# A gated cross-attention and feed-forward network on one core: the opening of stage 0 rearranged, and every product of stage 6 put into a fixed order

## The chip, the cores and the metric

The kernel runs on one core of one Trainium2 chip. The metric is device microseconds for one execution. The core's engines are called here as the profile calls them: PE is TensorE (matrix products and transposes), PEld its weight loads, DVE VectorE, ACT ScalarE, POOL GpSimd, SP SyncE, which here only issues DMAs. Each engine runs its own instructions in order; semaphores tie them together. PSUM, where products land, has eight banks of 128 x 512 float32.

## What is computed

The input x is 4 batches of 512 rows of 512 numbers, with a context of 4 x 512 rows of 256. Four pairs of blocks, eight stages (0 to 7), are added to x one after the other, each gated by tanh of a number:

```
x = x + tanh(g_xattn[0]) * L0_xattn(layernorm(x), ctx)     # stage 0
x = x + tanh(g_ffn[0])   * L0_ffn(layernorm(x))            # stage 1
...
x = x + tanh(g_xattn[3]) * L3_xattn(layernorm(x), ctx, pos) # stage 6
x = x + tanh(g_ffn[3])   * L3_ffn(layernorm(x))            # stage 7
```

Stage 0 is an attention with 16 heads of 32. Queries come from x, keys and values from the first 496 rows of the context, and queries and keys are normalized head by head. The last 16 rows of the context have weights of their own and a softmax of their own (the short context), and both results are added:

```
q = _ln((x @ Wq + bq).reshape(b, s1, H, HD), qn_w, qn_b)
k = _ln(kv[..., :HD], kn_w, kn_b)
ctx = _attn(q, k, v)
ctx_dca = _attn(q, k_dca, v_dca)        # 16 rows
return (ctx + ctx_dca) @ Wo + bo
```

Stage 6 is an attention with 32 heads of 16 over 512 context rows, with rotary positions on queries and keys, and an output product.

## The kernel before

Everything is float32 but for small helpers; the rows of x stay in SBUF for the whole run, as 16 tiles of 128 x 512. The stages follow each other; `tile_blocks_kernel` (L1873) opens a set of buffer pools for each.

**Who decides the order.** The code emits instructions in one order. A scheduler then places each engine's instructions when the kernel is built, by priority (what is emitted earlier, or under `high_priority`, comes first) and by its own idea of when inputs are ready. `tie` (L244) is the kernel's own means against that: a tied product may not be placed ahead of the tied product emitted before it. `together` (L253) emits a group of products, tied, to run side by side in different row or column groups of PE's array; the first of them may be made to wait for other instructions (`after`), so that the group starts as a whole. A `chain` (L235) is a sum of products into one bank; it is tied only if told so.

**Stage 0** (`s0`, L272). First the loads: SP issues, in the order of the code, the gates' numbers, the context of batch 0, the weights for keys and values (`wkv`), their bias, `wq`, `bq`, the short context's weights `wd` and bias, `wo`, `bo`, small rows, and six vectors of 32 numbers (`nw32`). The 16 tiles of x are issued by ACT (L70). `centre` (L319) subtracts from each head's weights their mean, on DVE, so that the normalization needs no mean. A product of `nw32` (L306) spreads the normalization's weights over the partitions.

`pieces(b)` (L351) lists the preparation of a batch: `kv` (four steps: keys and values of 128 rows), `xT` (layernorm and transposes of x), `turned` (transposes of normalized keys or queries), `query` (two steps), and `short` and `shortT` (logits, softmax and transposes of the short context). `second` (L490), called by batch 0's `short`, makes the short context's keys (`kbd`) and values (`vbd`). For batch 0 all pieces stand before the attention; for later batches they are dealt out over the slots of the batch before.

`maxima` (L555) is a generator. Each step gives a pair of products whose row maximum DVE takes (`after`); a head group of four heads and 512 queries takes eight steps. LEAD = 12 steps run ahead, as pairs (L681). Then each of the 32 slots of a batch (L685) joins two logit products (`pl`), the next pair of maxima (`ps`), a correction by the maxima, an exponential on ACT, and, one slot later, products with the values (`av`) or the sums (`sm`). The pool `sc` has two buffers of two banks, `pl` one of two banks, `av` and `sm` one bank each.

**Stage 6** (`s6`, L1534) is built in the same way, with 64 slots for each batch: two `pl`, two `ps`, and half of a step of `av` (`weigh`, L1687). After the last `av` of a head group ACT copies it out, and `norm` (L1710) transposes and scales it; after the last group `project` and `projected` make the output rows. `turn` (L1630) transposes the maxima into spare rows of the queries. `results`, `xT`, `query`, `queryT` are the next batch's preparation; `results` adds stage 5's outcome to x, which is 32 long additions on DVE in all. Banks come from two rings, four of `sc` and three of `pl`; `dealt` (L1553) remembers the reader of a bank for the groups, while `bank` (L1563) deals without remembering it. Only the groups of `together` are tied; transposes and chains are free.

Of the kernel before, what the change touches and what calls it, by code (L numbers as in the profile page):

```python
# [48 lines left out]
class Net:  # L49


    def __init__(self, ctx, tc, a):
# [10 lines left out]
        nc.sync.dma_start(self.gx, a["g_xattn"].partition_broadcast(P))  # L63
        nc.sync.dma_start(self.gf, a["g_ffn"].partition_broadcast(P))

        self.x = []
        for b in range(NB):
            for t in range(b * TB, (b + 1) * TB):
                xt = self.const.tile([P, D], F32, name=f"x_{t}")
                nc.scalar.dma_start(xt, a["x"][t * P : (t + 1) * P, :])  # L70
                self.x.append(xt)
# [39 lines left out]
        nc.scalar.activation(self.gx, self.gx, AF.Tanh)  # L111
        nc.scalar.activation(self.gf, self.gf, AF.Tanh)
# [45 lines left out]
    def evict(self, i, out, in_):  # L158

        if i % 2:  # L160
            self.nc.scalar.copy(out, in_)  # L161
        else:
            self.nc.vector.tensor_copy(out, in_)
# [60 lines left out]
    def transposed(self, name, src, dst, i=0, tied=False, room=None):  # L224

        pt = (room or self.mm)(f"ptr_{name}")
        for c in range(4):
            ins = self.nc.tensor.transpose(  # L228
                pt[:, c * P : (c + 1) * P], src[:, c * P : (c + 1) * P], self.ident
            ).ins  # L230
            if tied:
                self.tie(ins)
        self.evict(i, dst, pt.rearrange("p (c n) -> p c n", c=4))
# [38 lines left out]
    def s0(self):  # L272
# [8 lines left out]
        nc.sync.dma_start(wkv, a["s0_wkv"].rearrange("(c p) n -> p c n", p=P))  # L281
        bk = self.bcast("s0_bk", a["s0_bkv"][0:512])
        nc.sync.dma_start(wq, a["s0_wq"].rearrange("(c p) n -> p c n", p=P))
        bq = self.bcast("s0_bq", a["s0_bq"])
        nc.sync.dma_start(wd, a["s0_wd"].rearrange("(c p) n -> p c n", p=P))
        bd = self.t("s0_bd")
        nc.sync.dma_start(bd, a["s0_bd"][0:512].partition_broadcast(P))
        nc.sync.dma_start(wo, a["s0_wo"].rearrange("(c p) n -> p c n", p=P))
        bo = self.bcast("s0_bo", a["s0_bo"])
        fixed = lambda name, shape, dtype=F32: self.gp.tile(shape, dtype, tag=name, name=name)  # L290
# [4 lines left out]
        nc.vector.tensor_tensor(bvs[:, 0, :], bvs[:, 0, :], bvs[:, 1, :], op=ALU.add)  # L295
        bv = bvs[:, 0, :]

        nw32 = fixed("s0_nw32", [HD, 6])
        for i, k in enumerate(("qn_w", "qn_b", "kn_w", "kn_b", "kn_dca_w", "kn_dca_b")):
            nc.sync.dma_start(nw32[:, i : i + 1], a[k].rearrange("(p o) -> p o", o=1))  # L300
# [4 lines left out]
        pn = self.sc("s0_pn")[:, 0, 0:6]  # L305
        nc.tensor.matmul(  # L306
            pn, lhsT=rep.rearrange("p r m -> p (r m)"), rhs=nw32, start=True, stop=True
        )
        nw = fixed("s0_nw", [P, 6])
        nc.vector.tensor_copy(nw, pn)  # L310
        nc.vector.tensor_scalar(nw[:, 0:2], nw[:, 0:2], HD**-0.5, None, op0=ALU.mult)
# [20 lines left out]
        centre("wq", wq.rearrange("p c (h d) -> p c h d", d=HD))  # L332
        centre("bq", heads(bq))
# [17 lines left out]
        def pieces(b):  # L351
# [15 lines left out]
            def kv(k):  # L367
# [3 lines left out]
                for i in range(2):  # L371
                    self.chain(
                        pkv[:, i, :],
                        [
                            (cx[:, c, k * P : (k + 1) * P], wkv[:, c, i * 512 : (i + 1) * 512])
                            for c in range(CC)
                        ],
                    )
# [4 lines left out]
                if k == TB - 1:  # L383
                    normed(f"s0k_{b}", heads(room["k"]), room["vk"])
# [36 lines left out]
            def query(y):  # L421
# [21 lines left out]
                if y == 1:  # L443
                    normed(f"s0q_{b}", heads(room["q"]), room["vq"])

            def short():

                if b == 0:
                    second()
# [22 lines left out]
            def shortT():  # L472
# [7 lines left out]

            return (
                [lambda k=k: kv(k) for k in range(TB)]
                + [lambda y=y: xT(y) for y in range(2)]
                + [lambda y=y: turned("k", y, kT, 2) for y in range(2)]
                + [lambda y=y: query(y) for y in range(2)]
                + [lambda y=y: turned("q", y, qT, 0) for y in range(2)]
                + [short, shortT]
            )

        def second():  # L490


            n = NB * ND
            cd = fixed("s0_cd", [P, CC, NB, ND])
            for c in range(CC):
                nc.sync.dma_start(
                    cd[:, c],
                    a["ctxT"][c * P : (c + 1) * P, :].rearrange("p (b n) -> p b n", b=NB)[:, :, M:S],
                )
            centre("wd", wd[:, :, 0:512].rearrange("p c (h d) -> p c h d", d=HD))  # L500
            centre("bd", heads(bd))
            pk = self.sc("s0_pkd")[0:n, 0, :]
# [3 lines left out]
            kd = self.t("s0_kd")[0:n]  # L506
            va = self.s("s0_vd", H)[0:n]
            nc.vector.tensor_tensor(kd, pk, bd[0:n], op=ALU.add)
            squares("s0d", kd, va, n)
            normed("s0d", heads(kd), va, n)  # L510
            pt = self.sc("s0_ptd")[:, 0, 0 : 4 * n].rearrange("p (g b k) -> p b g k", g=4, b=NB)
            for g in range(4):
# [3 lines left out]
                    self.ident[0:n, 0:n],  # L516
# [23 lines left out]
            vbd = fixed("s0_vbd", [P, NB, D])  # L540
            for b in range(NB):
                pv = self.sc(f"s0_pvd_{b}")[:, 0, :]
                self.chain(
                    pv,
                    [
                        (cr[:, c, b].rearrange("p r k -> p (r k)"), wd[:, c, 512:1024])
                        for c in range(CC)
                    ],
                )
                nc.vector.tensor_tensor(vbd[:, b, :], pv, mask, op=ALU.mult)  # L550
            made["kbd"], made["vbd"] = kbd, vbd

        maxT = {}

        def maxima():  # L555

            freed = []
# [19 lines left out]
            for b in range(NB):  # L577
                kT, qT = made[b][0:2]
                for g in range(4):
                    nmx = self.s(f"s0_nmx_{b}_{g}", 16, "s0_nmx")  # L580
                    for t in range(TB):
                        for y in range(2):
# [3 lines left out]
                            ps = self.sc(f"ps_s0_{b}_{g}_{t}_{y}")  # L586
# [88 lines left out]
        for b in range(NB):  # L675
            stats[b] = self.lnstats(f"s0_{b}", self.x[b * TB : (b + 1) * TB], b)
            if b == 0:
                for piece in pieces(0):
                    piece()
        beside = maxima()  # L680
        for _ in range(LEAD):  # L681
            parts, freed, after = next(beside)
            self.together(parts, freed)
            after()
        for b in range(NB):  # L685
            kT, qT = made[b][0:2]
            todo = pieces(b + 1) if b + 1 < NB else []
# [730 lines left out]
    def rope(self, name, ps, t, out):  # L1418

        nc = self.nc  # L1420
# [3 lines left out]
        for i in range(2):  # L1424
# [3 lines left out]
            nc.vector.tensor_tensor(dst, x[:, 0, :, :], (cos, sin)[i], op=ALU.mult)  # L1428
            nc.vector.tensor_tensor(dst, dst, tmp, op=(ALU.subtract, ALU.add)[i])

# [12 lines left out]
    def headsT(self, name, r, y, pt):  # L1443

        v = r.rearrange("p (g h) k -> p g (h k)", g=8)
        for i in range(4):
            self.nc.tensor.transpose(pt[:, i * P : (i + 1) * P], v[:, 4 * y + i, :], self.ident)
# [86 lines left out]
    def s6(self):  # L1534
# [18 lines left out]
        def dealt(name, tag="sc"):  # L1553
            at = len(readers[tag])
            readers[tag].append(None)
            old = readers[tag][at - banks[tag]] if at >= banks[tag] else None
            t = self.ps3.tile([P, S], F32, tag=tag, name=f"s6_{name}", bufs=banks[tag])
            return t, (tag, at), [old] if old is not None else []

        def read(where, ins):  # L1560
            readers[where[0]][where[1]] = ins
# [434 lines left out]
```

## Time and profile before

| | us |
|---|---|
| median of 3 runs | 3382.92 (3382.7 to 3385.21) |
| the profiled execution | 3387.32 |
| its span | 3385.4 |
| first product of PE | starts at 32.27 |
| first product of keys (`s_pkv`) | 32.75 |
| first query product (`s_pq`) | 57.81 |
| first maxima (`ps_s`) | 111.39 |
| first logits (`pl_s`), stage 0 | 132.68 |
| batches 0, 1, 2, 3 of stage 0 begin | 132.68, 274.76, 434.55, 592.35 |
| stage 6 | about 2254 to 3003 |

The profile is of one execution, 4.4 us longer than the median of the runs. Times in a timeline are microseconds from the start of the span, then the duration; in square brackets stands the idle time of the engine before the instruction, and what ended it. A line with "x4" is four instructions merged. One float32 product appears as two records. In the table of windows each engine has its busy time and the number of its instructions, then come the granted clock of PE (1.00 is full), the share of the DMA engines' time, and GB/s. `s_` in front of a name is the stage's prefix with its number left out, so stage 0 and stage 6 both have an `s_po`.

### The profile page before, as it was taken

The numbers are of one execution on the slowest core, as the hardware profiler recorded it, in microseconds if no ns is written. First come the engines' busy times: TensorE is split into PE (matmuls) and PEld (weight loads), VectorE is DVE, ScalarE is ACT, GpSimd is POOL, SyncE is SP. The second block draws the span as 40 slices with busy tenths as digits, with TensorE's granted clock in tenths as the row PEclk, the third lists the DMA queues.
The fourth block names the chain that finished last, engine by engine and source line by source line (L and its number), as shares of the span: only waits on it lengthen the run. The fifth ranks groups of instructions, "written<-read, shape, count | busy, mean of one in ns | idle before, by whom it ended". The sixth has DMA issues, their size and how long they took to land.

```text
span 3385.4 us, 41976 instructions
## 1 busy us (share of the span) xinstructions
PE 2917.4 (86%) x15644; PEld 1452.6 (43%) x15648; DVE 1972.4 (58%) x3132; ACT 1196.0 (35%) x1927; POOL 626.0 (18%) x509
## 2 busy tenths in 40 slices
PE   4889898967998889998845699978999999989994
PEld 2333333223444444443423588853333333254673
DVE  5555555548898988886678311138656566634103
ACT  2243333355554454433322111113545444520231
POOL 0000000005564655660000122210000000000351
PEclk9799999988998999999967699987999999999997
DMA  3000000047676886861222599971000000022698
GB/s 126 7 1 7 1 1 9 1 157 223 197 230 183 235 231 194 235 207 61 79 72 73 183 320 324 323 272 47 14 27 13 27 1 1 1 75 78 247 385 315
DMA packets 266346, 438.69 MB, mean 130 GB/s; under 512 B 32368, under 2 KB 114544, under 8 KB 264608
## 3 DMA queue, kind: packets, MB, share of 16 engines
q1 hardware_dynamic: 247776, 382.52, 35.9%
q0 software_dynamic: 13760, 45.10, 3.7%
q10 hardware_dynamic: 4608, 8.39, 0.7%
q8 instruction: 125, 2.05, 0.3%
q14 instruction: 77, 0.63, 0.1%
HBM read 370.79 MB, written 65.13 MB: 129 GB/s over the span
## 4 chain that ended last, share of the span: by engine, by line
PE 37%; DVE 7%; issue 4%; ACT 2%; POOL 2%; DMA 2%; SPq 0%; POOLq 0%; ACTq 0%; DVEq 0%
PE s_po L238 8%; PE s_pl L262 8%; PE pg_s L238 6%; PE s_av L262 2%; PE s_pq L238 2%; PE s_ps L262 2%; ACT pr_s L1786 2%; PE s_ph L238 2%; POOL s_ys L1321 1%; DMA s_y<-s_ys 1%; DVE x L729 1%; DVE s_top L1670 1%; POOL s_xb L1294 1%; PE s_pr L238 1%; PE s_pkv L238 1%
## 5 line engine op out<-in xcount | busy, mean ns | idle before, releaser
L1012 POOL TENSOR_TENSOR s_h<-s_h,s_C 128x512 f32<-128x512 f32 x256 | 445.4, 1740 | 298.8 <-DVE s_h L1011 260.3
L1670 DVE TENSOR_REDUCE s_top<-s_ps 128x1 f32<-128x512 f32 x512 | 328.8, 685 | 164.1 <-PE s_ps L262 163.8
L1786 ACT ACTIVATE pr_s<-s_pl 128x512 f32<-128x512 f32 x512 | 277.9, 595 | 327.3 <-PE s_ps L262 293.7
L1011 DVE TENSOR_TENSOR_SCAN s_h<-s_da,s_db 128x512 f32<-128x512 f32 x256 | 311.9, 1218 | 60.1 <-PE s_y L262 34.3
L262 PE MATMUL s_pl<-s_qT,s_kT 32*128 32x512 f32 x1024 | 295.7, 653 | 29.8 <-DVE s_top L1670 11.7
L262 PE MATMUL s_ps<-s_kT,s_qT 32*128 32x512 f32 x1024 | 301.4, 674 | 4.5 <-DVE s_top L1670 4.5
L1010 ACT ACTIVATE s_da<-s_rdl,s_A 128x512 f32<-128x512 f32 x256 | 184.3, 722 | 330.3 <-DVE s_h L1011 327.0
L238 PE MATMUL s_ph<-xT_s,s_wu 128*128 128x256 f32 x1024 | 249.6, 399 | 0.7 <-ACT xT_s L161 0.7
L771 PE MATMUL s_acc<-s_wd,s_hT 128*128 128x512 f32 x512 | 239.9, 612 | 6.8 <-ACT s_hT L802 6.8
L262 PE MATMUL s_av<-pr_s,s_v 128*32 128x256 f32 (+2 forms) x2560 | 238.7, 445 | 0.2
L238 PEld LDWEIGHTS s_ph<-xT_s,s_wu 128*128 128x128 f32 x1024 | 199.3, 199 | 78.1 <-issue 47.7
L238 PEld LDWEIGHTS pg_s<-s_xbT,s_w 128*128 128x128 f32 (+1 forms) x1872 | 214.2, 184 | 19.8 <-issue 17.8
L599 DVE TENSOR_REDUCE s_nmx<-ps_s 128x2 f32<-128x992 f32 x128 | 151.4, 1184 | 116.6 <-PE ps_s L262 116.6
L238 PE MATMUL pg_s<-s_xbT,s_w 128*128 128x128 f32 (+1 forms) x1872 | 215.8, 276 | 1.4 <-ACT s_xbT L161 1.4
L1009 DVE TENSOR_TENSOR s_db<-s_B,s_rdu 128x512 f32<-128x512 f32 x256 | 205.6, 803 | 12.5 <-DMA s_B<-s_bc 4.9
L714 ACT ACTIVATE pr_s<-pl_s 128x1024 f32<-128x1024 f32 (+1 forms) x128 | 130.9, 1023 | 192.1 <-PE pl_s L262 161.7
L262 PE MATMUL s_y<-s_h,ident 64*64 64x512 f32 x1024 | 147.6, 640 | 50.6 <-issue 35.2
L1400 DVE TENSOR_TENSOR g_s<-g_s,pg_s 128x256 f32<-128x256 f32 x78 | 27.5, 352 | 263.8 <-ACT g_s L1399 263.8
L262 PE MATMUL pl_s<-s_qT,s_kT 32*128 32x512 f32 (+1 forms) x512 | 151.1, 668 | 26.1 <-ACT pr_s L714 23.0
L262 PE MATMUL ps_s<-s_kT,s_qT 32*128 32x496 f32 x512 | 156.2, 713 | 4.5 <-DVE s_nmx L599 4.1
L771 PEld LDWEIGHTS s_acc<-s_wd,s_hT 128*128 128x128 f32 x512 | 93.5, 192 | 151.8 <-issue 115.8
L1294 POOL DMA_INDIRECT s_xb<-s_xs,s_from x86 | 83.2, 967 | 378.4 <-PE ptr_s_xb L228 232.4
(376 smaller groups left out, 4264.5 us busy)
## 6 DMA issues: line engine op xcount, KB each, us to landing
s_B<-s_bc SPq DMA_DIRECT2D x256, 256.0 KB
s_C<-s_bc SPq DMA_DIRECT2D x256, 256.0 KB
s_w<-in_s_wg SPq DMA_DIRECT2D x39, 704.0 KB
s_w<-in_s_wu SPq DMA_DIRECT2D x39, 704.0 KB
s_w_rt<-in_s_ru SPq DMA_DIRECT2D x47, 512.0 KB
s_w_rt<-in_s_rd SPq DMA_DIRECT2D x47, 512.0 KB
s_w<-in_s_wd SPq DMA_DIRECT2D x39, 512.0 KB
s_y<-s_ys SPq DMA_DIRECT2D x32, 512.0 KB
```

Source lines behind the costliest of these rows:

```text
L238: ins = self.nc.tensor.matmul(out, lhsT=l, rhs=r, start=(i == 0), stop=(i == len(pairs) - 1)).ins
L262: ins = self.nc.tensor.matmul(out, lhsT=l, rhs=r, **flags).ins
L599: i = nc.vector.tensor_reduce(nmx[:, at : at + 2], ps[:, :, 0:M], axis=AX.X, op=ALU.max, negate=True,)
L714: nc.scalar.activation(prs[i][0:n], pl[0:n], AF.Exp)
L771: ins = nc.tensor.matmul(accs[i][t], lhsT=hT[:, j, t * P : (t + 1) * P], rhs=wd[f // 4][:, f % 4, :], start=(f == 0), stop=(f == FC - 1),).ins
L1009: nc.vector.tensor_tensor(db, br, du, op=ALU.mult)
L1010: nc.scalar.activation(da, dl, AF.Exp, scale=am[:, e, n : n + 1])
L1011: nc.vector.tensor_tensor_scan(h, da, db, 0.0, op0=ALU.mult, op1=ALU.add)
L1012: nc.gpsimd.tensor_tensor(h, h, cr, op=ALU.mult)
L1294: self.nc.gpsimd.indirect_dma_start(out=t, out_offset=None, in_=self.sorted[name][1], in_offset=bass.IndirectOffsetOnAxis(ap=fr[:, j : j + ...
L1670: ins = nc.vector.tensor_reduce(dst[:, i], ps[i][0], axis=AX.X, op=ALU.max, negate=True).ins
L1786: ins = nc.scalar.activation(prs[i][:, j, :], pl[j][0], AF.Exp).ins
```

## The change

In stage 0:

- x is loaded by SP instead of ACT, batch by batch, among the weights: the order is now the context, K's half of `wkv`, its bias, V's half, x of batch 0, `wq`, `bq`, the six vectors, `wd`, the short context's columns, x of batch 1, `wo`, small rows, the gates, x of batches 2 and 3. The gates' tanh goes to `gates`, after that.
- The centring of `wq` and the product of `nw32` become pieces after the four `kv` steps, and batch 0's `kv` chains and that product are tied.
- The normalization of keys and queries is done in halves (`half`), each as soon as two of the four steps are there.
- `second` keeps only the short context's keys before the maxima. Their transposes (`keys`), the four value chains (`values`), and batch 0's `short` and `shortT` become pieces of batch 0's loop.
- The lead of 12 maxima runs as six groups of four heads, two of them in `pl`'s buffer, with one wait for the group.

In stage 6:

- All transposes, query chains (but for batch 0's) and output chains are tied.
- Every deal of a bank remembers its readers, and a group waits for the readers of all banks that it and its neighbours had before (`before`), not for each product's own.
- Three empty pieces follow `results`; `turn`'s addition gets high priority on DVE.

The core of the diff:

```diff
+    def load(self, b):
+        for t in range(b * TB, (b + 1) * TB):
+            self.nc.sync.dma_start(self.x[t], self.a["x"][t * P : (t + 1) * P, :])
+
+    def gates(self):
+        for t, k in ((self.gx, "g_xattn"), (self.gf, "g_ffn")):
+            self.nc.sync.dma_start(t, self.a[k].partition_broadcast(P))
+            self.nc.scalar.activation(t, t, AF.Tanh)
...
-        nc.sync.dma_start(wkv, a["s0_wkv"].rearrange("(c p) n -> p c n", p=P))
-        bk = self.bcast("s0_bk", a["s0_bkv"][0:512])
+        for i in range(2):
+            half = slice(512 * i, 512 * (i + 1))
+            nc.sync.dma_start(
+                wkv[:, :, half], a["s0_wkv"][:, half].rearrange("(c p) n -> p c n", p=P)
+            )
+            if i == 0:
+                bk = self.bcast("s0_bk", a["s0_bkv"][0:512])
+        self.load(0)
         nc.sync.dma_start(wq, a["s0_wq"].rearrange("(c p) n -> p c n", p=P))
         bq = self.bcast("s0_bq", a["s0_bq"])
...
+        self.gates()
+        for b in range(2, NB):
+            self.load(b)
...
-                if k == TB - 1:
-                    normed(f"s0k_{b}", heads(room["k"]), room["vk"])
+                if k % 2:
+                    half("k", k // 2)
...
             return (
                 [lambda k=k: kv(k) for k in range(TB)]
+                + ([weights, lambda: statistics(0), first] if b == 0 else [])
+                + [lambda: turned("k", 0, kT, 2)]
                 + [lambda y=y: xT(y) for y in range(2)]
-                + [lambda y=y: turned("k", y, kT, 2) for y in range(2)]
+                + [lambda: turned("k", 1, kT, 2)]
                 + [lambda y=y: query(y) for y in range(2)]
-                + [lambda y=y: turned("q", y, qT, 0) for y in range(2)]
-                + [short, shortT]
-            )
+                + ([second] if b == 0 else [])
+                + [lambda y=y: turned("q", y, qT, 0) for y in range(2)],
+                [short, shortT],
+            )
...
+        todo, rest = pieces(0)
+        for piece in todo:
+            piece()
+        for b in range(1, NB):
+            statistics(b)
+        alone = [True]
         beside = maxima()
-        for _ in range(LEAD):
-            parts, freed, after = next(beside)
-            self.together(parts, freed)
-            after()
+        for _ in range(LEAD // 2):
+
+            two = [next(beside) for _ in range(2)][::-1]
+            self.together([p for parts, _, _ in two for p in parts], lead[-2:-1])
+            for _, _, after in two:
+                after()
+        alone[0] = False
+        rest = [keys, lambda: values(0)] + rest + [lambda b=b: values(b) for b in range(1, NB)]
...
         def dealt(name, tag="sc"):
-            at = len(readers[tag])
-            readers[tag].append(None)
-            old = readers[tag][at - banks[tag]] if at >= banks[tag] else None
+
             t = self.ps3.tile([P, S], F32, tag=tag, name=f"s6_{name}", bufs=banks[tag])
-            return t, (tag, at), [old] if old is not None else []
...
+            readers[tag].append([])
+            return t, readers[tag][-1].append
+
+        def before(tag):
+
+
+            old = readers[tag][-2 - banks[tag] - 2 : -banks[tag]]
+            return [r[-1] for r in old if r]
...
-            out = [results, lambda: xT(0), lambda: xT(1)]
+            out = [results] + 3 * [lambda: None] + [lambda: xT(0), lambda: xT(1)]
...
-            po = bank(f"pt_{b}_{g}")
+            po, read = dealt(f"pt_{b}_{g}")
             for t in range(TB):
                 ts = slice(t * P, (t + 1) * P)
-                nc.tensor.transpose(po[:, ts], oT[:, ts], self.ident)
+                self.flip(po[:, ts], oT[:, ts], True)
...
-                        self.together(parts + more, freed + pl[0][2] + pl[1][2])
+                        self.together(parts + more, freed + before("pl"))
```

`flip` is a transpose that is tied when told so.

## The prediction

> **What bounds the kernel now.** I read the page's first two parts, then the table of windows over the two stages that the diff touches, then the timelines of their seams.
>
> ```profile
> PE 2917.4 (86%) x15644; PEld 1452.6 (43%) x15648; DVE 1972.4 (58%) x3132; ACT 1196.0 (35%) x1927; POOL 626.0 (18%) x509
> ```
> ```profile
> core 0: us, PE busy (x) PEld busy (x) DVE busy (x) ACT busy (x) POOL busy (x), PEclk, DMA share, GB/s
> 0.00:32.20 32.20, 0.00 (x0) 0.00 (x0) 20.70 (x42) 3.46 (x6) 4.33 (x44) 1.00 0.87 310
> 57.80:111.40 53.60, 36.51 (x114) 19.78 (x114) 21.19 (x27) 10.11 (x15) 1.97 (x3) 0.78 0.00 0
> 111.40:132.70 21.30, 18.93 (x57) 6.21 (x56) 14.18 (x18) 1.01 (x1) 0.00 (x0) 0.50 0.00 1
> 2340.00:3003.00 663.00, 634.92 (x4628) 222.22 (x4624) 392.77 (x681) 312.99 (x580) 0.56 (x3) 0.99 0.03 11
> ```
> TensorE is the bound on the whole, but for the first 32.2 us it does nothing; from 57.8 to 111.4 it is busy for 36.5 of 53.6 us; in stage 6 it is busy throughout, so there only a better packing can gain. The timelines show what each stretch waits for:
>
> ```profile
> 14.81 1.20 DVE L325 TENSOR_REDUCE ce_wk<-s_wkv 128x32 f32<-128x1024 f32 x1
> ...
> 30.37 0.31 SPq L300 DMA_DIRECT2D s_nw<-in_kn_dca_b  x1
> 32.27 0.56 PE L306 MATMUL s_pn<-s_nw,s_rep 32*128 32x6 f32 x2 [32.27 <-DMA s_nw<-in_kn_dca_b]
> ```
> The first product is a tiny one. It waits for six tiny loads queued last behind megabytes, and all keys and values wait behind it.
>
> ```profile
> 2395.64 0.70 PE L262 MATMUL s_pl<-s_qT,s_kT 32*128 32x512 f32 x2
> 2395.65 0.70 PE L262 MATMUL s_ps<-s_kT,s_qT 32*128 32x512 f32 x2
> ...
> 2396.71 0.64 PE L262 MATMUL s_av<-pr_s,s_v 128*32 128x256 f32 x8
> 2397.72 1.13 PE L262 MATMUL s_pl<-s_qT,s_kT 32*128 32x512 f32 x4 [0.37 <-DVE s_top L1670]
> 2398.78 0.33 PE L1716 MATMUL s_pt<-ident,s_oT 128*128 128x128 f32 x1
> 2399.04 1.13 PE L262 MATMUL s_ps<-s_kT,s_qT 32*128 32x512 f32 x4
> 2400.09 0.55 PE L1716 MATMUL s_pt<-ident,s_oT 128*128 128x128 f32 x3
> ```
> In stage 6 a whole slot starts two pl and two ps products together (four row groups, 1.05 us). In a broken one an untied transpose (pt, from norm) sits in the middle: pl alone 1.06, ps alone 1.06. Counting the PE timeline from one start of s_av to the next: 142 plain slots of 1.83 us on average; 27 broken with pt of 3.90, against 2.29 for the three with pt that stayed whole; three with po and broken of 6.69 against 5.27 whole; three with ptx of 8.6 to 11.1.
>
> **Stage 0, until the maxima.** The loads up to K's half of wkv are 1.05 MB. The first x tile (0.26 MB) let DVE start at 4.84; at the 0.39 MB/us of the early DMA slices the rest comes 2.0 later: 6.9. Centring takes 1.20+0.16+1.20, so keys and values begin at 9.5 instead of 32.75. They last 16.0 as before: 25.5. All loads are now issued by SP: ten issues up to wq at about 0.4 are 4 us, hidden under 4 MB of data (0.393 MB/us came on SP's queue alone at 27 to 29 us, so one queue is no slower than two; ACT loses the 16 issues that held it until 20.5). The six tiny loads move ahead of wd and land near 15, before the product that needs them stands in line at 25; cd's two (32 KB, 0.65 to issue each) move ahead of x 1. Without that cover each would hold TensorE as before.
>
> The second limit is DVE, which had 32 idle microseconds for work that now falls beside the keys. After 9.5 it owes, from the rows of before: centring bk 1.5, four key steps of 1.38 (5.5), two half norms of about 1.45 (half of 0.55+2.29; 2.9), wq and bq 6.3, statistics 3.5, xl 2.0, one eviction 1.2; in all 22.9. So the query chain starts near 33, not 57.8. It lasts 14.0: 47. Its second half's norm (add, squares, reduce, root, reciprocal: 4.2 in the row of before, then 1.15 rather than 2.29) ends at 52.3, but the first two groups of maxima need only the first half: 52. ACT and DVE run in order, and gates (two Tanh, with their table loads of 1.28) and the statistics of x 1 to 3 now hang on the last loads, which land at 27 to 31. Stuck ahead of evictions they cost between 0 and 10 here; I take 3, since DVE is the limit until 33 anyway. Maxima begin at 55 instead of 111.4: **-56.5**.
>
> **The lead.** Twelve pairs took 21.3 us (1.66 per pair). Six groups of four wait for the reduce of pl's only buffer, 1.19, then run. The Trainium skill speaks here ("TensorE: Matmul & The Clock Gate", Part 1): after one busy window of about 3.4 us the clock is full. The row 111.4 to 132.7 says otherwise: granted 0.50 through 21 us with PE busy 89% of the time. By the rule a group takes 1.05+0.25+1.19, six take 15, and 6 us are gained; by the row 2.1+0.25+1.19, six take 21, nothing. I take the row: **0**.
>
> **What moves into the first loop.** Keys, four value chains, short and its transposes no longer stand before the maxima; they are seven more pieces among the 20 slots of batch 0. Batches 1 and 2 already show short and shortT beside the loop: the slot with ld takes 5.99 instead of 2.5, the next one 1.0 more, the slot with ptw 10.47, because TensorE waits 3.2 for the softmax chain and the pairs fall apart. That is 12 us, as much as the serial form cost (99.05 to 111.4). Values: 1.72 for each chain plus some 0.3, 8; keys 2. Their DVE work (four multiplies of 0.69, kbd 2.21, two copies of 0.75) fits DVE's 61 idle microseconds in this loop, and the mask (0.52+1.51) stays on an idle POOL. Bounds: 12 if only PE's own time counts (0.7+6.9+3.5+1), 30 if each of seven pieces breaks a slot by another 1.1. I take 22: **+22**.
>
> **Halved norms.** Each batch after the first has four roots instead of two between exponentials, each with two table loads (1.28) and 0.35 on ACT, 2.9. In before such an episode left PE idle for 1.2 where a piece covered it and 3.9 where none did. The six added ones stand before kv (3.7 of PE) and query (7): 0 to 17; I take 3. The shorter multiply takes off some of the three waits of 1.6 before ptk: -2. **+1**.
>
> Stage 0: -33.5. What was hidden there stays hidden: x 1 to 3 are first read after 55.
>
> **Stage 6.** All products in order of emission: norm's four transposes now follow directly on the last weigh, and must wait for ACT's copy of av.
>
> ```profile
> 2374.07 1.09 ACT L1786 ACTIVATE pr_s<-s_pl 128x512 f32<-128x512 f32 x2 [0.72 <-PE s_ps L262]
> 2374.14 0.64 PE L262 MATMUL s_av<-pr_s,s_v 128*32 128x256 f32 x8
> 2375.05 0.59 ACT L1707 COPY s_oT<-s_av 128x512 f32<-128x512 f32 x1
> ```
> The copy stands behind two exponentials and ends 1.5 after av starts, where the next group would start at 0.7. Behind the waiting transposes stands everything on PE. So the slot becomes 1.83+0.46+0.85 = 3.15, not 2.29: the tie gives back half of what it gains. 27x0.75 = -20; five norms without a ps partner lose 0.85: +4; three po slots -4; three ptx slots -13 (the pauses after results give xl time). The other group waits replace waits of the same products; distances shrink where a transposed query deals two tiles (0.1 to 0.2 on twelve), and results' stretch at 2300 to 2340 stays DVE's (18 to 19 busy in 20). Reserve +4. **-29**, bounds -10 and -60.
>
> **Sum**: -33.5-29 = -62.5 on the profiled execution's 3387.3 (span 3385.4 and 1.9 around it): 3324.8. The median of the runs, 3382.9, lies 4.4 lower, so I forecast 3320.
>
> **Rivals.**
> - *Everything is hidden.* norm's copy gets ahead of the exponentials, so slots fall to 2.29 (-27.5 more); the moved pieces cost bare PE time (-10); the lead runs at full clock (-6): 3277. For it: the three whole pt slots. Against: ACT's queue order in the row above.
> - *The new opening waits for its last loads*: Tanh or statistics stand ahead of evictions (+7), the roots cost the uncovered price (+14), stage 6 keeps half (+14): 3355 to 3360. For it: the 3.9 us waits.
> - *Slower*: in-order products make PE wait for its newest input. 126 tied pieces (norm, turn 32 each, xT 6, query and queryT 12 each, project and projected 16 each) need more than 0.5 us of new wait each, beyond norm's, to eat 62.5; at 0.6 it is 3320+76 = 3396. For it: norm itself waits 0.85. Against: the others come a slot (1.8) or more after their source.
> - *No change*: the first product starts early but the query chain stays where it is, and stage 6 trades one wait for another: 3380.
>
> **Chances.** Forecast's case 0.56 (3300 to 3342), all hidden 0.20, late loads 0.18, slower 0.04, no change 0.02. The range 3283 to 3352 leaves out about half of each side case. What this kernel's measurement can tell from no change is about 0.2% (7 us): faster 0.94, same 0.02, slower 0.04.
>
> **What would show it.** First pkv near 9.5, first pq near 33, first ps near 55, first pl near 76; ACT without a long wait for gates. A first pq beyond 40 makes the step on DVE wrong. Batch 0's loop near 164 instead of 142. In stage 6 no pt between pl and ps, pt's slots near 3.1: 2.3 would make the stall wrong, 3.9 the gain.

## The result, and the profile after

The changed kernel takes 3343.07 us (median of 4 runs, 3335.79 to 3345.06) beside 3383.98 for the kernel before: a ratio of 0.9875 [0.9858, 0.9892], 41 us less. The forecast was 3320, its range 3283 to 3352; 3343 is inside the range, just above the 3300 to 3342 that the forecast gave to its own case. The profiled execution took 3345.06 with a span of 3343.2, 42.3 less than the profiled execution before.

In the table of windows of the changed kernel, the first row is the same stretch as before; the others are the lead of maxima, and stage 6 from its first maxima to its last logits.

```profile
core 0: us, PE busy (x) PEld busy (x) DVE busy (x) ACT busy (x) POOL busy (x), PEclk, DMA share, GB/s
0.00:32.20 32.20, 18.85 (x48) 8.71 (x49) 23.18 (x46) 8.01 (x14) 4.33 (x44) 0.98 0.88 288
54.54:76.62 22.08, 14.18 (x61) 5.29 (x61) 16.34 (x23) 3.75 (x6) 0.00 (x0) 0.66 0.00 0
2269.60:2934.70 665.10, 599.01 (x4720) 207.96 (x4724) 432.74 (x783) 320.42 (x592) 0.00 (x0) 0.98 0.05 15
```

The same stretch of stage 6 in the kernel before:

```profile
2291.40:2978.90 687.50, 649.52 (x4721) 224.69 (x4722) 432.59 (x789) 320.90 (x594) 0.00 (x0) 0.97 0.05 15
```

PE works for 18.85 of the first 32.2 us, where it did nothing before. In stage 6 it is now busy for 599 of 665 us, where it was busy for 650 of 687.5. So the products are packed better (51 us less busy time, a few of them the clock's, see below the table), and more than half of what that saved has become waiting (66 us idle instead of 38). The opening's timeline:

```profile
7.32 1.22 DVE L342 TENSOR_REDUCE ce_wk<-s_wkv 128x32 f32<-128x1024 f32 x1 [7.32 <-DMA s_wkv<-in_s_wkv]
...
10.53 8.78 PE L238 MATMUL s_pkv<-s_wkv,ctx_s 128*128 128x512 f32 x16 [10.53 <-DVE s_wkv L344]
...
26.81 0.38 PE L238 MATMUL s_pn<-s_nw,s_rep 32*128 32x6 f32 x2
...
36.62 13.90 PE L238 MATMUL s_pq<-s_wq,s_xT 128*128 128x512 f32 x32
```

The first keys start at 10.53, the tiny product (`s_pn`) stands behind them without a wait, and the query follows at 36.62. A slot of stage 6 with norm's transposes, from one start of s_av to the next:

```profile
2318.80 0.64 PE L262 MATMUL s_av<-pr_s,s_v 128*32 128x256 f32 x8
2318.89 1.08 ACT L1846 ACTIVATE pr_s<-s_pl 128x512 f32<-128x512 f32 x2 [0.72 <-PE s_ps L262]
...
2319.86 0.59 ACT L1765 COPY s_oT<-s_av 128x512 f32<-128x512 f32 x1
...
2320.51 0.66 PE L1495 MATMUL s_pt<-ident,s_oT 128*128 128x128 f32 x4 [1.06 <-ACT s_oT L1765]
```

In all 30 slots with pt and ps the four products of the group now start together, but s_pt waits 1.06 for a copy that stands behind two exponentials on ACT. The list of PE's waits in stage 6 (what waited, for what; us in total, times, longest) gives it as the largest by far:

```profile
PE s_pt L1495 <- ACT s_oT L1765: 29.7, 28, 1.1
PE s_ps L262 <- DVE s_top L1728: 5.8, 4, 1.9
PE s_pl L262 <- ACT pr_s L1846: 5.7, 28, 0.6
PE s_pl L262 <- DVE s_top L1728: 4.0, 4, 1.3
```

The largest line of the same list for the kernel before:

```profile
PE s_pl L262 <- DVE s_top L1670: 11.7, 28, 0.8
```

Nearly all of it stood in the broken slots (one stands in the prediction's timeline, at 2397.72). All lines together are 26.1 us before and 55.7 after.

By stretches of the two profiled executions (us):

| stretch | before | after | difference | forecast |
|---|---|---|---|---|
| up to the first maxima | 111.4 | 54.5 | -56.9 | -56.5 |
| the lead | 21.3 | 22.1 | +0.8 | 0 |
| loop of batch 0 | 142.1 | 164.7 | +22.6 | +22 |
| loops of batches 1 to 3, to stage 1's first product | 446.4 | 449.8 | +3.4 | +1 |
| stage 0 in all | 721.2 | 691.1 | -30.1 | -33.5 |
| stage 6, first maxima to last logits | 687.6 | 665.1 | -22.5 | -29 |
| everything else | 1976.6 | 1987.0 | +10.4 | 0 |

The last line is at least in part scatter. Of the 10.4, stage 1's long stretch has 6.3 (755.4, then 761.7). The kernel with the same stages 0 and 1 but the old stage 6 (first experiment) has 754.1 there, and the twelve kernels below, none of which touches that stretch, lie between 754.0 and 760.7. So single executions differ by some 8 us there, and the two of the table happen to have the shortest and the longest "everything else" of all fourteen profiled executions (1976.6 and 1987.0). The other kernels with the changed stage 0 have 1978.2 to 1986.8, so a few us may be the change's; that was not isolated.

The line of stage 6 needs care as well. Three kernels have stage 6 as it was: the kernel before, and two of the experiments. It takes 687.6, 686.1 and 680.5 us in them. Five kernels have the changed stage 6 as it is, and there it takes 665.1 to 667.5. The granted clock of PE tells the first three apart. The first row below is a stretch in the middle of stage 6 in the kernel before, the second is the same stage in the kernel with 680.5 (the six vectors first), from 2330 to its last logits:

```profile
2678.70:2685.50 6.80, 6.80 (x29) 3.22 (x29) 2.12 (x4) 1.66 (x3) 0.00 (x0) 0.50 0.00 0
2330.00:2966.30 636.30, 611.90 (x4573) 212.83 (x4576) 390.31 (x681) 310.68 (x577) 0.00 (x0) 1.00 0.04 11
```

The kernel before has three such stretches at half clock there, 13.6 us together, and a slot with ptx that falls in part into one takes 11.13, where the same slot takes 9.47 in the other kernel. The changed kernel has none (1.00 from 2312 to its last logits). At half clock products take about twice as long (a group of four 2.04 instead of 1.11, last section), so half of the 13.6 is lost: about the 7 us between 687.6 and 680.5. So of the 22.5 us some 7 are a matter of how the clock fell in one execution, and the change is worth about 15 in stage 6. Below, each edit is read in its own stretch beside the medians.

### The profile page after: what moved, and what is told of

Same layout as the page of the kernel before. It is cut to its first block, busy times and chain, and to the rows that moved or that the text cites. A ratio compares the mean times of both kernels' runs of the same rounds, so it can differ in the third digit from the quotient of the medians.

```text
span 3343.2 us, 42023 instructions
## 1 busy us (share of the span) xinstructions
PE 2877.5 (86%) x15644; PEld 1440.6 (43%) x15648; DVE 1972.4 (59%) x3148; ACT 1215.7 (36%) x1948; POOL 629.3 (19%) x509
## 3 DMA queue, kind: packets, MB, share of 16 engines
q8 instruction: 124, 2.03, 0.3%
## 4 chain that ended last, share of the span: by engine, by line
PE 37%; DVE 7%; ACT 4%; issue 3%; POOL 2%; DMA 2%; POOLq 0%; DVEq 0%; ACTq 0%
PE s_po L238 8%; PE s_pl L262 8%; PE pg_s L238 6%; ACT pr_s L1846 3%; PE s_ph L238 2%; PE s_pq L238 2%; PE s_av L262 1%; DVE x L772 1%; DMA s_y<-s_ys 1%; PE s_pr L238 1%; PE s_pkv L238 1%; PE pt_s L217 1%; POOL s_ys L1364 1%; PE s_pb L238 1%; DVE st_s L174 1%
## 5 line engine op out<-in xcount | busy, mean ns | idle before, releaser
L262 PE MATMUL s_ps<-s_kT,s_qT 32*128 32x512 f32 x1024 | 291.4, 661 | 7.8 <-DVE s_top L1728 5.8
L1052 DVE TENSOR_TENSOR s_db<-s_B,s_rdu 128x512 f32<-128x512 f32 x256 | 202.7, 792 | 13.6 <-DMA s_B<-s_bc 5.9
L262 PE MATMUL pl_s<-s_qT,s_kT 32*128 32x512 f32 (+1 forms) x512 | 154.2, 680 | 26.1 <-ACT pr_s L757 23.0
```

The costliest lines, as they stand in the source:

```text
L262: ins = self.nc.tensor.matmul(out, lhsT=l, rhs=r, **flags).ins
L1052: nc.vector.tensor_tensor(db, br, du, op=ALU.mult)
```

## Experiments

My theory was the prediction's: the two halves of the change are separate, stage 0 is bounded by the path through DVE until the maxima, and in stage 6 the tie of norm's transposes takes back about as much as it gives, because they wait for ACT. The rivals: the moved pieces or the added roots are what costs, and the common wait of a group is what keeps the groups whole. In each entry the ratio is to the kernel before, run on the same chip; the changed kernel's is 0.9875.

**Each half alone.** One kernel has the changed stage 0 and stage 6 as before, the other the reverse.

> Stage 0 of the changed kernel, stage 6 of the kernel before. If the two parts add up, this run is 30 us faster than the kernel before (stage 0 ends at 691 in its trace instead of 721) and its stage 6 takes the 688 us of before between its first maxima and its last logits. The stretch from stage 1's first up-product to its last accumulation grew from 755 to 762 us in the changed kernel's trace, and the router-to-blocks tail by 2. If stage 0's change causes that (other buffers, other times), it stands at 762 here too and the run is only 23 us faster; if it is scatter between executions, it lies anywhere between 754 and 763.

> Stage 6 of the changed kernel, stage 0 of the kernel before. If the parts add up: 21 us faster than the kernel before, all of it between the first maxima and the last logits of stage 6 (665 us instead of 688), and stage 0 ends at 721 as before. If stage 6 gained only because it began at another moment of the clock's throttling, it stays near 680. Stage 1's stretch: 755 if stage 0's change caused the 762, anywhere if it is scatter.

Stage 0 alone: 3357.29 (3347.53 to 3359.65), 0.9914 [0.9899, 0.9929]. Stage 6 alone: 3371.02 (3366.25 to 3381.94), 0.996 [0.9946, 0.9975]. Beside the 3384.5 of the kernel before in these runs they gain 27.2 and 13.5, together 40.7 of the 41: within the scatter the halves do not touch each other. By the stretches they would gain more: 31.4 in stage 0 (689.8) and 20.2 in stage 6 (667.4, beside 687.6). Beside the 680.5 of a stage 6 without the half clock it is 13.1, and that agrees with the median. So stage 6 did not gain only by the moment at which the clock fell, but a third of what the two traces show is that.

**Norm one slot later.**

```diff
                 nc.scalar.copy(oT, avs[g])
+                behind(lambda: None, more=True)
                 behind(norm, b, g, oT, more=True)
```

> The changed kernel, but norm's four transposes are emitted one slot after the copy of av instead of in the same slot. My theory: in the changed kernel the tie makes all of TensorE wait for that copy, 1.07 us in each of 30 slots; a slot later the copy is long done, the slots with pt fall from 3.34 to about 2.29, and the kernel is 30 us faster than the changed one (near 3312). The rival: the 1.07 is the price of the group's wait for DVE's readers, not of the copy. Then the slots with pt stay at 3.3 or the wait moves to the slot after, and the time stays at 3343.

3308.05 (3304.03 to 3313.81), 0.9769 [0.9753, 0.9785]: 36 us less than the changed kernel by the ratios, as expected. Its timeline around the same transposes:

```profile
2319.10 0.59 ACT L1765 COPY s_oT<-s_av 128x512 f32<-128x512 f32 x1
...
2319.85 0.64 PE L262 MATMUL s_av<-pr_s,s_v 128*32 128x256 f32 x8
...
2320.42 0.66 PE L1495 MATMUL s_pt<-ident,s_oT 128*128 128x128 f32 x4
```

The copy is done before the next s_av starts, and s_pt follows without a bracket: no wait. The 30 whole slots with pt last 2.26 on average instead of 3.34, and stage 6 takes 636.8 instead of 665.1. That is 28.3 less, and the wait that it removed was 29.7. (The rest of the 36 lies outside stage 6, mostly in stage 1's stretch: 754.0 beside 761.7.) The waits for exponentials, 5.7 us in 28 places, are gone too (0.7, once): most of them had stood in the slot behind a stall. So the tie cost what it did by the position of the tied instruction.

**Ties without the common wait.** `before` gives no readers, so each product waits only for the reader of its own bank; the ties stay.

```diff
-            return [r[-1] for r in old if r]
+            return []
```

> The changed kernel, but no group of stage 6 waits as a whole: each product waits only for its own bank, and the ties stay. If the ties do the work and the wait only stands in for waits of the same products, it stays within 5 us of the changed kernel (3338 to 3348). If the common wait is what keeps the four products side by side, pl starts ahead of ps in many slots, each of them costs up to 1.05 us more, and with a quarter of some 200 slots that is 50 us slower (3390).

3325.47 (3322.49 to 3326.95), 0.9822 [0.9807, 0.9838]. Neither expectation holds: it is faster, by 18 us. PE's waits in stage 6 of this kernel:

```profile
PE s_pt L1495 <- ACT s_oT L1765: 25.2, 28, 1.1
PE s_ptq L1495 <- DVE s_q_r L1473: 2.1, 1, 2.1
PE s_ps L262 <- DVE s_top L1728: 1.5, 5, 0.5
```

The waits of s_pl for the exponentials and for DVE are gone, and s_ps waits 1.5 in all instead of 5.8. There is a price: in most slots the first product of pl now starts alone, and the other three follow.

```profile
2385.45 0.86 PE L262 MATMUL s_pl<-s_qT,s_kT 32*128 32x512 f32 x2
2385.62 0.70 PE L262 MATMUL s_ps<-s_kT,s_qT 32*128 32x512 f32 x2
```

Of 140 plain slots, 37 start their four products together and take 1.66 on average; 76 start them some 0.17 apart and take 1.83; 27 start them more than 0.2 apart and take 2.17. The changed kernel has 140 together, at 1.88. The stretch of stage 6 goes from 665.1 to 654.7, so 10 us are the common wait's, about half of it in the slots with pt (3.19 instead of 3.34). The rest of the 18 lies where the edit does not reach, mostly in stage 1's stretch (754.0 beside 761.7). I had read the common wait as a mere replacement of each product's own. In the kernel before, too, a group waited as a whole, for those readers of its own banks that `dealt` remembered; so this run shows what a common wait costs, not what the change added to it.

**Own banks only.** Two kernels tell apart the two readings of that: that a group waits for the slowest of its own banks, or that it waits for two banks more (those dealt just before its own). One has the smaller wait, the other has it together with the later norm.

```diff
-            old = readers[tag][-2 - banks[tag] - 2 : -banks[tag]]
+            old = readers[tag][-2 - banks[tag] : -banks[tag]]
```

> The changed kernel with a group waiting only for the last readers of its own banks, not for those of the two banks dealt before them as well. If the common wait costs because every product waits for the slowest of the group's own banks, nothing changes: 3340 to 3347, stage 6 at 665. If it costs because of the two extra readers, it goes to where the kernel without a common wait is: 3325, stage 6 at 655. My theory is the first, because the two extra readers are the older ones.

> Norm one slot later and the common wait only for the group's own banks. With the theory of the run of own banks alone (extra readers cost nothing) it is the same as norm later: 3304 to 3312. With the other it lies at 3290, as norm later without any common wait.

3350.28 (3338.13 to 3352.11), 0.9891 [0.9875, 0.9908], stage 6 at 667.1; and with norm later 3313.26 (3309.55 to 3316.13), 0.9776 [0.976, 0.9793], stage 6 at 635.8. Neither differs from its partner with the larger wait (0.9875 and 0.9769). The medians lie a little above what I wrote, but so does the kernel before in these runs (3387.2). The extra readers cost nothing that can be seen, which leaves the group's own slowest bank.

**Both edits of stage 6.** Norm later, and no common wait.

> The changed kernel with both edits of stage 6 that gained by themselves: norm one slot later and no common wait of a group. Norm later took 35 us off (3308), no common wait 18 (3325). If the two costs are different ones (the transposes' wait for ACT's copy, and a pair held back for the other pair's banks) they add: 3290, stage 6 at 626. If the common wait only cost what it added in the slots that norm's wait had upset, little is left of it: 3303 to 3310.

3301.58 (3296.67 to 3302.86), 0.9742 [0.9726, 0.9758], the best of all. By the ratios it lies 0.0027, or 9 us, below norm later alone, with stage 6 at 629.5 beside 636.8. So 7 to 9 of the common wait's 10 us remain when the slots with pt no longer stall, and perhaps all: this trace has two stretches of 3.4 us at a granted clock of 0.50 in the middle of stage 6, and that of norm later alone has none. Neither expectation was met: the costs are mostly different ones, but the 18 that I added were too many, since some 8 of them were never stage 6's.

**Without the pauses after results.**

```diff
-            out = [results] + 3 * [lambda: None] + [lambda: xT(0), lambda: xT(1)]
+            out = [results] + [lambda: xT(0), lambda: xT(1)]
```

> The changed kernel without the three empty pieces after results. My forecast booked -13 for three ptx slots that wait for xl (8.6 to 11.1 us each before), with the pauses as the reason. Then without them the tied transposes of x wait for xl with everything behind them: three times 3 to 6 us, 3352 to 3361. If it is the tie or the order that gained them, and not the pauses, it stays at 3340 to 3347.

3358.25 (3347.98 to 3361.51), 0.9903 [0.9884, 0.9922]: 9.5 us more by the ratios, 15 more in the stretch of stage 6 (680.2) of the profiled execution, which is the slowest of the four. The six slots with ptx take 46.5 us together, and four of them again carry an output product as well. In the changed kernel the six take 17.3, and the four output products add 13.6 to slots of their own, 30.9 in all. In two of the six, ptx waits 1.40 and 0.73 for xl. Against these 15.6 stand 8 us gained in other slots; and some 7 are lost at the end of the stage, where plain groups take 2.08 instead of 1.13:

```profile
2933.70:2951.50 17.80, 17.80 (x71) 4.41 (x69) 0.68 (x2) 5.43 (x10) 0.00 (x0) 0.50 0.00 1
```

No pause stands near there, so the medians' 9.5 is the better figure for the pauses. They do pay for that part of the stage, by less than the 15.

**Whole norms in stage 0.** K's norm is made after the fourth step and the query's after its second half, so there are two roots for each batch again.

```diff
-                if k % 2:
-                    half("k", k // 2)
+                if k == TB - 1:
+                    normed(f"s0k_{b}", heads(room["k"]), room["vk"])
...
-                half("q", y)
+                if y == 1:
+                    normed(f"s0q_{b}", heads(room["q"]), room["vq"])
```

> The changed kernel with the norms of keys and query undivided again (two roots for each batch instead of four, the multiplies whole). My forecast priced the halving at +1: three for the six added roots, less two for shorter waits ahead of the transposed keys. So undoing it changes nothing that can be told: ratio to the changed kernel within 0.3%, 3334 to 3351 beside 3343, the sqrt table loads of stage 0 back from 25 to 13. The rival of the forecast (the added roots cost their uncovered price) expects 10 to 17 us less: 3326 to 3333. In the opening the second half's norm then stands ahead of the first maxima: first ps 1 to 3 us later than 54.5.

3359.74 (3355.63 to 3362.52), 0.9923 [0.99, 0.9945]. The opposite of both expectations on the time: 17 us slower, though ACT's table loads in the loops fell from 25 to 13 as written (those for roots from 12 to 6). The first maxima start at 64.61 instead of 54.54, with PE idle for 5.43 before the transposes of the query (1.14 before the maxima in the changed kernel); the lead gives 4 of this back. Batch 0's loop takes 171.6 instead of 164.7, batch 1's 163.6 instead of 160.2. Batch 1 shows how, first in this kernel:

```profile
299.33 1.28 ACT L358 ACT_TABLE_LOAD   x1
...
302.29 1.02 ACT L758 ACTIVATE pr_s<-pl_s 128x1024 f32<-128x1024 f32 x1
302.54 2.29 DVE L360 TENSOR_TENSOR s_k<-s_k,s_vak 128x2048 f32<-128x2048 f32 x1
303.36 1.87 PE L262 MATMUL pl_s<-s_qT,s_kT 32*112 32x512 f32 x4 [3.66 <-ACT pr_s L758]
```

and at the same place in the changed kernel:

```profile
286.38 1.28 ACT L358 ACT_TABLE_LOAD   x1
...
286.68 1.09 PE L416 MATMUL s_ptk<-ident,s_k 128*128 128x128 f32 x8
...
289.14 0.38 PE L598 MATMUL s_ptm<-ident,s_split 128*128 128x128 bf16 x4 [1.37 <-DVE s_nmx L634]
...
290.38 1.19 PE L262 MATMUL pl_s<-s_qT,s_kT 32*112 32x512 f32 x2 [0.85 <-ACT pr_s L757]
```

While ACT loads its tables, the changed kernel transposes the half of K that is already normalized. With a whole norm those transposes depend on the very root that is being made, and nothing covers it: PE waits 3.66 there, and 1.37 and 0.85 in the changed kernel. Of the 17 us, 6 lie in the opening with its lead and 11 in the loops. The changed order of pieces needs the halves.

**The lead as twelve pairs.**

```diff
-        alone = [True]
+        alone = [False]
...
-        for _ in range(LEAD // 2):
-
-            two = [next(beside) for _ in range(2)][::-1]
-            self.together([p for parts, _, _ in two for p in parts], lead[-2:-1])
-            for _, _, after in two:
-                after()
+        for _ in range(LEAD):
+            parts, freed, after = next(beside)
+            self.together(parts, freed)
+            after()
```

> The changed kernel with its lead as twelve pairs in two row groups, as before, instead of six fours. My forecast took 0 for the lead, by the row of granted clock 0.50: 3340 to 3347, from first ps to first pl 21 to 23 us as in both kernels. The full-clock rule says the fours would have saved 6 us; they did not (22.1 against 21.3), so under it the pairs could only be slower, if the changed kernel's lead is held up by something else than the clock: 28 us for the lead and 3349.

3342.58 (3338.46 to 3343.31), 0.9873 [0.9851, 0.9894], the lead 21.5, the first logits at 79.47 (76.54 to 79.06 in the kernels that have the fours and nothing else moved in stage 0): no difference.

**The short context ahead of the maxima.** Keys, all values, the softmax chain and its transposes run before the lead, as before.

```diff
+        rest = [keys] + [lambda b=b: values(b) for b in range(NB)] + rest
+        for piece in rest:
+            piece()
         alone = [True]
...
-        rest = [keys, lambda: values(0)] + rest + [lambda b=b: values(b) for b in range(1, NB)]
+        rest = []
```

> The changed kernel with keys, the four value chains, the short context and its transposes ahead of the maxima again (nothing of it in batch 0's loop). By my sum the moved pieces cost 22 us in the loop (it went from 142.1 to 164.7); the serial form costs 12 for the softmax chain and its transposes, four value chains of 1.72 and keys of 1 to 2: 20 to 22. So the move itself is worth next to nothing: 3337 to 3350, with the first pl at 96 to 99 instead of 76.6 and batch 0's loop at 142 to 144. The rival, that the move is what the opening lives on, expects 10 to 20 us more: 3353 to 3363.

3345.75 (3341.64 to 3348.47), 0.9888 [0.9867, 0.9909], the same as the changed kernel. The first logits start at 100.39 instead of 76.62, and batch 0's loop takes 144.0 instead of 164.7: 23.8 later, and 20.7 given back. This part of the change moves 21 us from one place to another.

**The kernel before, with only the six vectors loaded first.**

> The kernel before with one thing changed: the six tiny vectors that the first product needs are loaded first of all instead of last. If those six loads alone held the opening, the first product comes as soon as its weights are centred: first keys and values by 18 to 20 instead of 32.75, and about 13 us of the 3384 go: 3371. My reading is that two limits stand one behind the other, and DVE's work ahead of the query (centring wq, statistics of all tiles) is the second: the start of the keys moves by 13, the start of the maxima by 0 to 8, so 3376 to 3384.

3376.58 (3371.2 to 3386.7), 0.9972 [0.9963, 0.9981]. Keys start at 22.62 instead of 32.75, the query at 52.08 instead of 57.81, the maxima at 103.18 instead of 111.39. Stage 0 ends at 715.7 instead of 721.2. Keys came later than the 18 to 20 that I wrote, because the statistics of ten tiles of x, and waits for their loads, stand ahead of the centring on DVE (its first reduction starts at 19.42). Six loads at the head of a queue, with nothing else moved, give 8 of the 57 us by which the maxima came forward.

## Why the prediction came out as it did

- **Stage 0 until the maxima (-56.5).** Measured -56.9. The parts were less exact, and that they add up so well is in part luck. Keys came at 10.53 instead of 9.5: K's half of the weights landed at 7.32 (6.9 forecast), and bk's reduction got in between on DVE. The query came at 36.62 instead of 33. DVE paused only once before it (1.71 us), and did 3.2 us of work that the forecast's list left out: the centring of the short context's weights and bias (`wd`, `bd`), which the scheduler placed ahead of the query although `second` is emitted behind it. The reserve of 3, booked for late gates and statistics, covered this; the gates themselves stopped nobody (Tanh ran at 36.95, while PE was in the query chain). That DVE is the second limit is shown by the run with the six vectors first: keys 10 us earlier, query only 6.
- **The lead (0).** Right: 22.1 and 21.3, and pairs do as well as fours. It was put down to the clock of 0.50 throughout, which is only half true: see the last section.
- **What moves into batch 0's loop (+22).** Right twice: the loop grew by 22.6, and taking the pieces out made it 20.7 shorter. That the serial form costs as much was also stated (12 for the chain, 1.72 for each value chain, keys), and is shown.
- **Halved norms (+1).** Against the kernel before it holds (+3.4 over three loops, of which a part is scatter). As a statement on halving it was wrong in sign: undoing it costs 17. I priced the added roots by the exposed episode (3.9) and the shorter multiply by 2, and did not ask what stands in the slot beside a root. In the kernel before, x's transposes did; in the changed order the other half's transposes do.
- **Stage 6 (-29).** Measured -22.5, of which some 7 are the half clock in the trace of before; about -15 without it. The stall was right in kind: "must wait for ACT's copy of av". It was too small, 0.85 forecast and 1.06 shown (28 waits, 29.7 us). The slots with pt went to 3.34 (3.15 forecast), so the 27 broken ones gave 15 instead of 20. The three po slots (5.27) gave 4 as booked, the ptx slots (2.68 to 3.10) 14, or 12 beside the stage without half clock (13 booked); the pt slots that had been whole, or had no ps, lost 4 as booked. The step that failed is "The other group waits replace waits of the same products" with its reserve of 4. Before, PE waited 26.1 us in this stage, 11.7 of it in one line that belongs to the broken slots, so 14.4 elsewhere. After, it waits 26.0 besides norm's 29.7. That is 11.6 of new waits, 5.7 of them for exponentials, mostly in the slots behind the stalls. Plain slots rose from 1.83 to 1.88 (1.80 in the stage without half clock). Without any common wait the stretch is 10 shorter.
- **The rest (0).** +10.4 in the profiled execution, mainly stage 1. The two kernels with half the change have 1979.5 and 1980.8 there, 3 and 4 above the kernel before, which has the lowest figure of all. How much of the 10.4 is scatter and how much the change's stays open.

From 3320 to 3343: 3.4 in stage 0, 6.5 in stage 6, about 10 in the part that was not touched, and some 3 in how the profiled execution stood to the median (4.4 above it before, 2.0 after). That the half clock in the trace of before took 7 us off what was missing in stage 6 is luck: beside the stage without it, 14 us are missing there. The rival in which in-order products make PE wait for its newest input was right about the mechanism, but in the main only for norm; the tied pieces that come a slot later hardly stalled (ptm waits 0.6 in all).

Not tried: whether norm later lets the pauses after results be shortened, a version of the best kernel with the serial short context, and what makes the clock fall in the middle of stage 6.

## What to carry to other kernels

When free instructions are put into a fixed order, ask of each what its newest input is: one tied directly behind its producer's slot cost a full wait here (28 times 1.06), one slot later it cost nothing. When work is moved in front of another step, look at which piece used to cover a table load or a root, and leave something independent in that slot. A common wait for a group costs what the slowest member waits. Here that was more than it saved: without it 103 of 140 groups came apart, most of them by 0.17 us, and the stage was 10 us shorter. And before a difference of a few us in one stage is read off two traces, compare the granted clock there.

## What the hardware showed that I had not expected

The first keys of the changed kernel run slower than the later ones although the column of the granted clock says 1.00 for both. Rows of the table of windows, the first two within the keys, the others within the lead:

```profile
10.53:13.90 3.37, 3.37 (x4) 1.51 (x5) 3.37 (x11) 0.00 (x0) 0.00 (x0) 1.00 1.05 391
13.90:18.30 4.40, 4.40 (x12) 1.92 (x11) 2.69 (x5) 1.58 (x2) 0.00 (x0) 1.00 0.63 182
...
61.30:65.70 4.40, 1.77 (x14) 0.34 (x8) 3.51 (x4) 1.64 (x2) 0.00 (x0) 0.89 0.00 0
65.70:70.00 4.30, 2.99 (x12) 1.03 (x16) 3.27 (x3) 0.00 (x0) 0.00 (x0) 0.50 0.00 0
```

Four records in 3.37 us are 0.84 each; the sixteen records of the next block of keys (7.20 from 19.68 on) are 0.45 each. Both have a granted clock of 1.00. So the first 3.4 us after standstill run at about half speed, and the column of the granted clock does not show it (it also says 1.00 for the first 32.2 us of the kernel before, where PE does nothing). The time fits the rule of the Trainium skill that the prediction weighed ("TensorE: Matmul & The Clock Gate", Part 1): full clock after about 3.4 us of activity. The lead is another thing: within it the granted clock itself falls to 0.50, and a group of four, 1.11 at 63.34, takes 2.04 at 65.72. In the kernel with whole norms the first three groups took 1.11 and the next two 2.03 and 2.04. (Its lead was 18.1 instead of 22.1 mostly because the query's second transposes, 2.1 us after a wait of 1.4, lie within the changed kernel's lead and ahead of that kernel's.) In the kernel with pairs it is 0.50 from the first pair on, with PE busy for 19.84 of 21.51 us. A busy PE did not bring the clock back within those 21 us, which the rule would have done; what sets the moment at which it falls was not isolated.
